# One product in four moved to TensorE in the middle layers of a four-layer state-space network

## The chip, the cores and the metric

The kernel runs on one core of one Trainium2 chip. The time is device microseconds of one execution of the whole program; three runs of the kernel before took 18013.67 to 18025.56 us, median 18020.86. The engines are named as in the profile: PE is TensorE (PEld its weight loads), DVE is VectorE, ACT is ScalarE, POOL is GpSimd, SP is SyncE, whose queue issues the DMAs.

## The reference

Four image layers on a batch of 4 images of 48 x 48 pixels and 192 channels, all in float32. Each holds selective scans. For a sequence of tokens t, channels d and N = 16 states n,

```
delta = softplus(dt @ dtW.T + dtB)
h[d,n] = exp(delta[d] * A[d,n]) * h[d,n] + (delta[d] * u[d]) * B[n]
y[d]   = sum over n of h[d,n] * C[n]      (+ D[d] * u[d])
```

Here u is the layer's input after a convolution, and dt, B and C are projections of it. Layers 0 and 3 are Mamba blocks with 384 channels, run forward and backward (layer 3 over every row and every column on its own, so that a scan starts anew every 48 tokens). Layers 1 and 2, the middle layers, run the scan over the whole image of 2304 tokens with 192 channels in four directions (rows, columns, and both reversed), add the four results, and normalize them.

## The kernel before

**Tiling.** A sequence is cut into chunks of CH = 384 tokens. One chunk of one direction of one image is a *job*; the middle layers have 2 x 4 x 4 x 6 = 192 jobs, of class DirJob (L536), all in one call of `run_jobs` (L1029). With 192 channels in blocks of 64, two halves of the states share the 128 partitions: partitions 0 to 63 hold 64 channels with states 0 to 7, partitions 64 to 127 the same channels with states 8 to 15 (`parts` = 2, `wide` = 64). So a job has 3 channel blocks i, and for each 2 *groups* g of NG = 4 states: 6 steps (i, g) a job, 1152 steps in the stage. Layers 0 and 3 use MambaJob (L588) with `parts` = 1: 12 steps a job.

**One step in the middle layers**, spread over engines and over neighbouring turns of the loop:

- *projection*: PE makes `bcd` (dt, B and C rows) from `xs`, ACT copies it, `spread` (L412) writes the 32 rows of B and C to DRAM (`bc`);
- *delta*: three PE products, each with a Softplus on ACT (`softplus`, L417);
- *fetch* (L422): SP loads the group's 4 B rows and 4 C rows back, each spread over 64 partitions, one DMA for each half: tile `bcb`, of which the pool holds 4;
- *decay* (L437): four Exp on ACT write `a` = exp(delta x A), into one of three buffers, two steps ahead;
- *drive* (L465): POOL makes `dus` = delta x xs; *enter* (L470): ACT copies it to `du` in PSUM, when a new i begins. In the middle layers it stands between the third and the fourth Exp of that turn;
- *carry* (L455): POOL copies the last state of the chunk before into the first column of the B rows, ahead of the product; `du` holds a 1 there;
- *scan* (L475): DVE multiplies `du` with the four B rows into `inputs` (PSUM, 4 x 385 elements a partition), and then runs the recurrence h = a x h + inputs over them in one scan instruction;
- *weigh* (L501): POOL copies the last column to `state` and multiplies h by the C rows, in place;
- *reduce* (L516): PE adds the four h to `y` in PSUM with a matrix of two stacked identities' sum (`pools.sum`); for a new i, `skip` (L561) first adds what the other directions left and D x u;
- *take* (L568), *gate* (L572), *close* (L577): ACT copies `y` to `yc`, PE adds its two halves to `ys`, ACT copies that to `o`, and after the third i SP stores it.

**Layers 0 and 3** differ in one thing that matters here: of the four products du x B of a group, MADE = 2 are made by PE (`fill`, L710). For that `du` is turned on PE (`turn`, L685, to `duT`), and the B row is brought in as a diagonal: `spread` (L641) writes the tokens of that row with 4-byte elements onto the diagonal of a zeroed DRAM block (`dg`), and `fetch` (L662) loads it to `bcb`. PE then multiplies `duT` by the diagonal blocks into PSUM tile `made`. DVE multiplies and scans only the other two states, and scans each made product with an instruction of its own, which takes its start from `state`.

**Order of the work.** DVE, POOL and PE execute in the order in which the program is written (`InOrder`), ACT through explicit dependencies (`in_order`). `run_jobs` writes that order: for each turn t it emits the scan of step t, decays of t+2, weigh of t, the next jobs' projections by slot (`stream`), the image ends' normalization by slot (`Side`: PE in slots 0, 4 and 5, POOL products in 0, 2, 4 and 5), gate, drive (of t+3 in the middle layers, t+4 in the others) and reduce. The number of a turn within its job is its slot, 0 to 5. In the middle layers reduce of t-1 is the last thing of a turn (`behind` = 1). `h` has 4 buffers, PSUM's eight banks hold `inputs` (4), `du`, `y` and two `ps` tiles for everything else.

Of the kernel before, what the change touches and what calls it, by code (L numbers as in the profile page):

```python
# [13 lines left out]
AF = mybir.ActivationFunctionType  # L14
# [7 lines left out]
Q = 96  # L22
CH = 384
# [5 lines left out]
MADE = 2  # L29
LINE = 3 * MADE * 128  # L30

# [30 lines left out]
class K:  # L62
# [100 lines left out]
    def mean_weights(self, n):  # L163
        w = self.tile(self.const, [Q, Q], f"mean{n}")
        self.nc.vector.memset(w, 1.0 / n)
        return w
# [82 lines left out]
class ScanPools:  # L249
# [6 lines left out]
    def __init__(self, k, ctx, parts, rows):  # L256
# [6 lines left out]
        self.made = parts == 1  # L263
# [9 lines left out]
        self.given = NG - MADE if self.made else NG  # L273
# [7 lines left out]
        if self.made:  # L281
            self.made_inputs = k.tile(self.vec, [128, 1024], "made")[:, 512 - CH : 512 + CH]
            self.n_jobs = 0
            self.diags = []
            zeros = self.decays[2].rearrange("p j l -> p (j l)")[:, : LINE + 1]
            k.g.memset(zeros, 0.0)
            for n in range(2 * self.groups):
                d = k.dram([128 * (LINE + 1)], "dg")
                k.nc.sync.dma_start(d.rearrange("(t x) -> t x", x=LINE + 1), zeros)
                self.diags.append(d)  # L290
# [41 lines left out]
class ScanJob:  # L332
# [16 lines left out]
    def turn(self, i):  # L349
        pass  # L350

    def turn_back(self, i):
        pass

    def fill(self, i, g):
        pass
# [55 lines left out]
    def spread(self):  # L412

        self.bc = self.k.dram([2 * N, self.pools.W], "bc")
        self.k.nc.sync.dma_start(self.bc, self.bcd[: 2 * N, :])

    def softplus(self, i, pd):  # L417
        if i == 0:
            self.delta = self.k.tile(self.pools.two, [128, 3, CH], "delta")
        self.k.act(self.delta[:, i, :], pd, AF.Softplus, bias=self.w.dtb[:, i, :])  # L420

    def fetch(self, g):  # L422

        k, pools = self.k, self.pools
        wide = pools.wide
        both = k.tile(pools.bcs, [128, 2, NG, pools.W], "bcb")
        self.bcb[g] = both[:, 0, :, :], both[:, 1, :, self.tokens]
        self.fetched[g] = []
        for m in range(pools.parts):
            at = (m * pools.groups + g) * 2 * NG  # L430
            ins = k.nc.sync.dma_start(
                both[m * wide : (m + 1) * wide].rearrange("p s j l -> p (s j l)"),
                self.bc[at : at + 2 * NG, :].rearrange("r l -> (r l)").partition_broadcast(wide),
            )
            self.fetched[g].append(ins)

    def decay(self, i, g, between=None):  # L437

        k, w, pools = self.k, self.w, self.pools
        if i == 0:  # L440
            self.fetch(g)
# [1714 lines left out]
```

## Time and profile before

| what | value |
|---|---|
| median of 3 runs | 18020.86 us |
| profiled execution | 18024.41 us, span 18022.6 us |
| busy share of the span | PE 90%, DVE 91%, ACT 76%, POOL 79% |
| granted TensorE clock, mean | 0.921 |
| middle layers, 6150 to 12135 us (5985 us) | PE 4672.44, DVE 5843.86, ACT 4359.13, POOL 4979.05 us busy; clock 0.80; DMA share 0.65 |
| ACT_TABLE_LOAD, 7000 to 11500 us | 2 x 143 of 1283 ns |
| delta on ACT, 7000 to 11500 us | 429 of 580 ns |

The shares of the whole span are a mean over stages with different limits: up to about 5.7 ms runs layer 0, then the input part of layer 1, from about 6.1 to 12.1 ms the scans of the middle layers, from 12.3 ms layer 3, and from about 17.3 ms the closing perceptron. The change is read from the middle stage.

A line of instruction groups holds the line of kernel.py, the engine, the operation, the tiles it writes and reads, shapes and count; behind the bar the busy time in us, the mean of one in ns, the idle time of the engine just before these instructions, and what ended most of that idle time. L59 is the helper that keeps program order, so groups are told apart by tiles. A line in order of time holds the start, the length, engine, line, operation and tiles, and in brackets idle time before it.

### The profile page before, as it was taken

What the parts mean: (1) busy time and instruction counts of PE and PEld (TensorE: products, weight loads), DVE (VectorE), ACT (ScalarE), POOL (GpSimd) and SP (SyncE); (2) the same over time, 40 slices, a digit from 0 to 9 for tenths busy, and PEclk for the clock granted to TensorE, in tenths of its full rate; (3) what the DMA queues carried; (4) which work ended last, traced back from release to release, by engine and by line L of the source; (5) the groups of instructions that cost most, each with busy time, mean ns of one, the idle gap of its engine ahead of it and who ended that gap; (6) DMA issues with size and microseconds to landing.
All of it is one profiled execution on the core that took longest, in us unless ns stands there. A gap on an engine that the chain in (4) does not pass through costs nothing. (4 is left out here: it accounts for less than half of the span.)

```text
span 18022.6 us, 313028 instructions
## 1 busy us (share of the span) xinstructions
PE 16243.2 (90%) x118512; PEld 10759.8 (60%) x118512; DVE 16418.0 (91%) x10747; ACT 13776.3 (76%) x25601; POOL 14149.0 (79%) x10862
## 2 busy tenths in 40 slices
PE   9999999999999777787777877878999999999999
PEld 7787787888885322222222222226888888888874
DVE  8899899999996799999999999996999999999992
ACT  7888888888885567777777777777888888888874
POOL 7877878878874488888888888876888888888880
PEclk9999999999999878788888887789999999999999
DMA  4343343333333466666666666663343343433431
GB/s 137 122 128 124 125 134 122 128 126 128 128 126 93 105 137 146 151 148 153 152 148 149 144 150 140 147 145 112 122 127 125 120 124 123 132 123 122 125 118 50
DMA packets 1229187, 2324.58 MB, mean 129 GB/s; under 512 B 704376, under 2 KB 962016, under 8 KB 1075232
## 3 DMA queue, kind: packets, MB, share of 16 engines
q1 hardware_dynamic: 1227680, 2304.55, 46.8%
q8 instruction: 938, 15.37, 0.4%
q14 instruction: 569, 4.66, 0.1%
HBM read 2105.57 MB, written 200.98 MB: 128 GB/s over the span
## 5 line engine op out<-in xcount | busy, mean ns | idle before, releaser
L59 POOL TENSOR_TENSOR h<-h,bcb 128x1536 f32<-128x1536 f32 x3456 | 11312.2, 3273 | 798.6 <-DVE h L59 499.1
L104 ACT ACTIVATE a<-delta,A 128x384 f32<-128x384 f32 (+1 forms) x13824 | 7377.6, 603 | 911.7 <-DVE h L59 901.2
L59 DVE TENSOR_TENSOR_SCAN h<-a,inputs 128x770 f32<-128x770 f32 (+2 forms) x3456 | 7915.9, 2290 | 146.5 <-DVE inputs L59 1.8
L59 DVE TENSOR_TENSOR inputs<-du,bcb 128x770 f32<-128x770 f32 (+2 forms) x3456 | 4256.4, 1232 | 287.2 <-POOL bcb L59 100.9
L59 PE MATMUL made<-bcb,duT 128*128 128x128 f32 x27648 | 3559.6, 279 | 172.1 <-DVE h L59 139.6
L59 PEld LDWEIGHTS y<-ident,h 128*128 128x128 f32 x27648 | 3119.8, 142 | 845.0 <-issue 485.7
L59 PE MATMUL y<-ident,h 128*128 128x128 f32 x27648 | 3508.5, 277 | 59.8 <-ACT yt L104 49.2
L59 PEld LDWEIGHTS made<-bcb,duT 128*128 128x128 f32 x27648 | 3341.4, 195 | 273.9 <-DVE h L59 178.7
L59 PE MATMUL y<-h,sum 128*64 128x384 f32 x9216 | 2661.7, 643 | 750.2 <-POOL h L59 547.4
L59 DVE TENSOR_TENSOR_SCAN h<-a,made 128x768 f32<-128x768 f32 (+1 forms) x1536 | 2343.2, 1536 | 263.2 <-PE made L59 256.4
L59 PEld LDWEIGHTS y<-h,sum 128*64 128x64 f32 x9216 | 848.7, 167 | 2175.9 <-issue 982.2
L59 DVE TENSOR_TENSOR_SCAN h<-a,state,made 128x384 f32<-128x384 f32 x1920 | 1827.8, 993 | 221.1 <-PE made L59 219.4
L59 POOL COPY state<-h 128x4 f32<-128x4 f32 x2304 | 434.4, 189 | 1908.5 <-DVE h L59 1879.5
L59 PE MATMUL ps<-bcd,dtT 12*128 12x384 f32 (+1 forms) x2304 | 1076.9, 580 | 245.1 <-ACT delta L104 240.2
L59 PE MATMUL ps<-u,inT 96*128 96x384 f32 x3456 | 1251.7, 489 | 38.8 <-DMA u<-xn_wh 27.1
L104 ACT ACTIVATE delta<-ps,vec 128x384 f32<-128x384 f32 x1152 | 636.4, 577 | 344.3 <-PE ps L59 338.2
L59 PEld LDWEIGHTS ps<-bcd,dtT 12*128 12x128 f32 (+1 forms) x2304 | 415.1, 206 | 808.8 <-ACT delta L104 487.3
L59 PE MATMUL ps<-yt,outT 128*96 128x384 f32 x2304 | 808.7, 488 | 0.4 <-POOL yt L59 0.4
L59 PE MATMUL ps<-xh,diag 32*32 32x192 f32 x32256 | 796.8, 324 | 4.0 <-ACT xc L104 2.3
L59 PEld LDWEIGHTS ps<-u,inT 96*128 96x128 f32 x3456 | 600.5, 191 | 304.0 <-issue 36.4
L104 ACT ACT_TABLE_LOAD x603 | 773.6, 1283 | 10.6
L101 ACT ACT_TABLE_LOAD x600 | 769.8, 1283 | 9.8 <-PEq L2146 0.7
(147 smaller groups left out, 15082.7 us busy)
## 6 DMA issues: line engine op xcount, KB each, us to landing
bcb<-bc SPq DMA_DIRECT2D x768, 770.0 KB
bcb<-bc SPq DMA_DIRECT2D x384, 1155.0 KB
bcb<-bc SPq DMA_DIRECT2D x384, 1152.0 KB
bcb<-dg SPq DMA_DIRECT2D x768, 384.0 KB
y<-o SPq DMA_DIRECT2D x192, 288.0 KB
xs<-xi_wh SPq DMA_DIRECT2D x96, 288.0 KB
xs<-xi_hw SPq DMA_DIRECT2D x96, 288.0 KB
added<-y SPq DMA_DIRECT2D x96, 288.0 KB
```

The source lines that it names most:

```text
L59: return lambda *a, **kw: self.tc.keep_in_program_order(op(*a, **kw))
L101: self.in_order(self.nc.scalar.preload_act_table_set(LOG_EXP))
L104: return self.in_order(self.nc.scalar.activation(out, in_, func, **kw))
```

## The change

In the middle layers PE makes one of the four products of each group (`MADE = {1: 2, 2: 1}`). The machinery of MambaJob (`spread`, `fetch`, `turn`, `fill`, `scan`) moves into ScanJob and is written for both values of `parts`. For a middle step this means:

- DVE multiplies and scans 3 x 385 elements instead of 4 x 385, and scans 384 made elements in a third instruction;
- PE turns the first 64 rows of `dus` (3 matmuls for each i) and makes the product with 6 matmuls of 128 columns (3 token blocks x 2 halves); reduce of t-1 is now followed by turn and then by fill of t+1; `inputs` takes three PSUM banks and `made` one;
- the fetch of a job's two groups is emitted two turns earlier (four steps ahead instead of two) and has a third DMA, the diagonal; `spread` writes one more row block and four diagonals;
- close, take and enter stand in front of the decays on ACT;
- the three deltas are copied with their bias and then go through one Softplus of 1152 elements, as in MambaJob;
- drive is emitted for t+4 instead of t+3; the result is copied into `added` (now three buffers) in place of `o`; `mean96` lives only in the input part of layer 1.

```diff
-MADE = 2
-LINE = 3 * MADE * 128
+MADE = {1: 2, 2: 1}
...
-        self.made = parts == 1
+        self.made = MADE[parts]
+        self.turned = parts == 1
+        self.line = 3 * self.made * parts * 128
...
-        self.given = NG - MADE if self.made else NG
+        self.given = NG - self.made
...
+        made = k.tile(self.vec, [128, 512 * self.made], "made")
+        at = 512 - CH if self.made == 2 else 0
+        self.made_inputs = made[:, at : at + self.made * CH]
...
     def spread(self):
-        self.bc = self.k.dram([2 * N, self.pools.W], "bc")
-        self.k.nc.sync.dma_start(self.bc, self.bcd[: 2 * N, :])
+        k, pools = self.k, self.pools
+        sync, parts, made = k.nc.sync, pools.parts, pools.made
+        n = parts * pools.groups * (pools.given + NG)
+        self.bc = k.dram([n, pools.W], "bc")
+        sync.dma_start(self.bc, self.bcd[:n, :])
+        be = k.dram([parts, pools.groups, made, CH], "be")
+        sync.dma_start(be.rearrange("m g e l -> (m g e) l"), self.bcd[n : 2 * N, self.tokens])
+        at = pools.n_jobs % 2 * pools.groups
+        pools.n_jobs += 1
+        self.lines = pools.diags[at : at + pools.groups]
+        for g in range(pools.groups):
+            line = self.lines[g].rearrange("(t x) -> t x", x=pools.line + 1)[:, : pools.line]
+            line = line.rearrange("t (b e m c) -> t b e m c", b=3, m=parts, c=128)
+            for e in range(made):
+                for m in range(parts):
+                    with k.nc.allow_non_contiguous_dma(reason="diagonal"):
+                        sync.dma_start(
+                            line[:, :, e, m, 0:1],
+                            be[m, g, e].rearrange("(b t v) -> t b v", t=128, v=1),
+                        )
 
     def softplus(self, i, pd):
...
-        self.k.act(self.delta[:, i, :], pd, AF.Softplus, bias=self.w.dtb[:, i, :])
+        k.act(self.delta[:, i, :], pd, AF.Identity, bias=self.w.dtb[:, i, :])
+        if i == 2:
+            k.act(self.delta, self.delta, AF.Softplus)
 
     def fetch(self, g):
...
+        k.nc.sync.dma_start(
+            t[:, n:], self.lines[g][: 128 * pools.line].rearrange("(t x) -> t x", t=128)
+        )
...
+    def turn(self, i):
...
+        for b in range(3):
+            k.t.matmul(
+                ps[:, b * wide : (b + 1) * wide],
+                self.du[i][:wide, b * 128 : (b + 1) * 128],
+                k.ident[:wide, :wide],
+                start=True,
+                stop=True,
+                is_transpose=True,
+                skip_group_check=True,
+            )
+        self.duT[i] = k.tile(pools.two, [128, 3, wide], "duT")
+        k.copy(self.duT[i].rearrange("p b d -> p (b d)"), ps)
+
+    def fill(self, i, g):
...
+        for b in range(3):
+            for e in range(pools.made):
+                at = e * CH + b * 128
+                for m in range(pools.parts):
+                    k.t.matmul(
+                        pools.made_inputs[m * wide : (m + 1) * wide, at : at + 128],
+                        self.duT[i][:, b, :],
+                        self.bcb[g][2][:, b, e, m, :],
+                        start=True,
+                        stop=True,
+                        skip_group_check=True,
+                    )
...
     def scan(self, i, g):
...
+        n = pools.given
+        du = pools.du.unsqueeze(1).to_broadcast([128, n, pools.W])
+        k.v.tensor_tensor(pools.b, du, self.bcb[g][0], ALU.mult)
...
+        scan(slice(0, n), slice(0, pools.W), pools.b.rearrange("p j l -> p (j l)"))
...
+        for e in range(pools.made):
+            at = g * NG + n + e
+            first = 0.0 if self.prev is None else self.prev.state[:, i, at : at + 1]
+            scan(
+                slice(n + e, n + e + 1),
+                self.tokens,
+                pools.made_inputs[:, e * CH : (e + 1) * CH],
+                first,
+            )
...
     def close(self, i):
-        if i == 0:
-            self.o = self.k.tile(self.pools.two, [64, 3, CH], "o")
-        self.k.copy(self.o[:, i, :], self.ys)
+        self.k.copy(self.added[:, i, :], self.ys)
...
-    behind = 2 if jobs[0].pools.made else 1
-    ahead, taken, gated, driven = 2, behind + 1, behind + 2, 2 + behind
+    behind = 2 if jobs[0].pools.turned else 1
+    ahead, taken, gated, driven = 2, behind + 1, behind + 2, 4
+    fetched = 2 * ahead if behind == 1 else ahead
...
-        coming = at_group(t + 1, 0)
-        if behind == 2:
-            if done := at_group(t - taken, last_group):
-                done[0].take(done[1])
-            if coming:
-                coming[0].enter(coming[1])
-                coming = None
+        if t + fetched < len(groups) and groups[t + fetched][1] == 0:
+            job, i, g = groups[t + fetched]
+            job.fetch(g)
+        if done := at_group(t - gated - 1, last_group):
+            done[0].close(done[1])
+        if done := at_group(t - taken, last_group):
+            done[0].take(done[1])
+        if coming := at_group(t + 1, 0):
+            coming[0].enter(coming[1])
         if t + ahead < len(groups):
             job, i, g = groups[t + ahead]
-            job.decay(i, g, (lambda: coming[0].enter(coming[1])) if coming else None)
-        if done := at_group(t - gated - 1, last_group):
-            done[0].close(done[1])
-        if behind == 1 and (done := at_group(t - taken, last_group)):
-            done[0].take(done[1])
+            job.decay(i, g)
...
-        if soon := at_group(t + 2, 0):
+        if behind == 2 and (soon := at_group(t + 2, 0)):
             soon[0].turn(soon[1])
...
         if 0 <= t - behind < len(groups) and behind == 1:
             job, i, g = groups[t - behind]
             job.reduce(i, g)
+        if behind == 1 and (soon := at_group(t + 2, 0)):
+            soon[0].turn(soon[1])
         if t + 1 < len(groups):
             job, i, g = groups[t + 1]
             job.fill(i, g)
```

## The prediction

> **What bounds the kernel now.** First the stretches of the span: busy time by engine (us and instructions, in the order PE, PEld, DVE, ACT, POOL), granted clock, DMA share, GB/s.
>
> ```profile
> 3000.00:4000.00 1000.00, 992.75 (x9001) 810.54 (x8999) 950.22 (x850) 837.24 (x1560) 797.13 (x760) 0.98 0.39 126
> 8000.00:9000.00 1000.00, 784.65 (x2484) 268.13 (x2484) 979.82 (x383) 732.64 (x1367) 841.95 (x721) 0.81 0.66 151
> 13000.00:14000.00 1000.00, 968.48 (x9845) 805.48 (x9843) 943.14 (x655) 816.37 (x1521) 864.51 (x436) 0.99 0.39 122
> ```
>
> Layers 0 and 3 (first and third row) are held by TensorE; they already make products there. The middle layers are held by VectorE, 98% busy. Next the groups of instructions by form, middle layers (7000 to 11500 us), then layer 0 (1000 to 5000 us).
>
> ```profile
> L59 POOL TENSOR_TENSOR h<-h,bcb 128x1536 f32<-128x1536 f32 x856 | 2948.4, 3444 | 69.5 <-POOL state L59 1.2
> L59 DVE TENSOR_TENSOR_SCAN h<-a,inputs 128x1540 f32<-128x1540 f32 x855 | 2873.6, 3361 | 32.9 <-DVE inputs L59 0.5
> L59 PE MATMUL y<-h,sum 128*64 128x384 f32 x6832 | 1971.0, 640 | 527.2 <-POOL h L59 374.0 <-POOL state L59 61.7 <-issue 42.9
> L59 DVE TENSOR_TENSOR inputs<-du,bcb 128x1540 f32<-128x1540 f32 x856 | 1515.2, 1770 | 78.8 <-POOL bcb L59 23.3 <-ACT du L104 13.7 <-PE y L59 12.2
> ```
>
> ```profile
> L59 POOL TENSOR_TENSOR h<-h,bcb 128x1536 f32<-128x1536 f32 x828 | 2410.8, 2912 | 66.8 <-POOL state L59 0.6
> L59 DVE TENSOR_TENSOR_SCAN h<-a,inputs 128x770 f32<-128x770 f32 x827 | 1453.0, 1757 | 30.1
> L59 DVE TENSOR_TENSOR_SCAN h<-a,state,made 128x384 f32<-128x384 f32 x1367 | 1301.4, 993 | 158.3 <-PE made L59 157.0
> L59 PE MATMUL made<-bcb,duT 128*128 128x128 f32 x9926 | 1290.9, 281 | 14.3 <-DVE h L59 11.2 <-DMA bcb<-dg 2.0
> L59 DVE TENSOR_TENSOR inputs<-du,bcb 128x770 f32<-128x770 f32 x828 | 797.1, 963 | 53.0 <-POOL bcb L59 52.3 <-DMA bcb<-bc 0.4
> ```
>
> The layer 0 rows are the price list of the new shape. Third, the order of time on VectorE, which shows what a mean hides: the distance from start to start. Middle layers, then layer 0:
>
> ```profile
> 8041.75 1.77 DVE L59 TENSOR_TENSOR inputs<-du,bcb 128x1540 f32<-128x1540 f32 x1
> 8043.55 3.36 DVE L59 TENSOR_TENSOR_SCAN h<-a,inputs 128x1540 f32<-128x1540 f32 x1
> 8046.95 1.77 DVE L59 TENSOR_TENSOR inputs<-du,bcb 128x1540 f32<-128x1540 f32 x1
> ```
>
> ```profile
> 3001.52 0.96 DVE L59 TENSOR_TENSOR inputs<-du,bcb 128x770 f32<-128x770 f32 x1
> 3002.51 1.76 DVE L59 TENSOR_TENSOR_SCAN h<-a,inputs 128x770 f32<-128x770 f32 x1
> 3004.19 1.89 DVE L59 TENSOR_TENSOR_SCAN h<-a,state,made 128x384 f32<-128x384 f32 x2
> 3006.01 0.96 DVE L59 TENSOR_TENSOR inputs<-du,bcb 128x770 f32<-128x770 f32 x1
> ```
>
> A quiet middle step is 8046.95-8041.75 = 5.20 us. The scan is followed 0.04 us after its end by the product that overwrites what it reads; in layer 0 the next instruction starts 0.08 before a scan's end (1.68 against 1.76). The stage has 1152 steps; from the first product at 6085.16 to the last at 12135.01 they took 6049.85/1151 = 5.256 each.
>
> Fourth, POOL in order of time, around its longest step:
>
> ```profile
> 8004.75 0.19 POOL L59 COPY state<-h 128x4 f32<-128x4 f32 x1 [0.41 <-PE y L59]
> 8005.02 3.45 POOL L59 TENSOR_TENSOR h<-h,bcb 128x1536 f32<-128x1536 f32 x1
> 8008.43 0.99 POOL L59 TENSOR_TENSOR nx<-nx,nsq 96x384 f32<-96x384 f32 x1
> 8009.38 0.99 POOL L59 TENSOR_TENSOR dus<-delta,xs 128x384 f32<-128x384 f32 x1
> 8010.32 0.18 POOL L59 COPY bcb<-state 128x4 f32<-128x4 f32 x1
> ```
>
> VectorE's products start at 8004.72 and 8010.55 here: the carry into bcb stands behind a norm's product and a drive, and the step grows to 5.83.
>
> **VectorE's own time.** Product: (1770-963)/770 = 1.048 ns an element, so 1155 elements take 963+385x1.048 = 1367 ns, plus the 0.03 gap: 1.40. Scan: (3361-1757)/770 = 2.083, so 2559 ns, less 0.08: 2.48. The scan of the made product: (3006.01-3004.19)/2 = 0.91. Sum 4.79, against 5.20: -0.41 a quiet step, -472 us over 1152. Measured from the mean of 5.256, which holds 0.06 of waits, a stage without any wait would save 537. That is the floor; the rest is what grows around it. (The chunk that opens a pass has no state, 935 ns in its row; left out, 0.01 a step.)
>
> **TensorE.** Added a step: 12 matmul instructions of 128 columns, and 3 turns every second step. PE is now busy 4672.44 us in 1138 steps (6150 to 12135), 4.11 each, at clock 0.80: 3.29 at full clock. Price of the 12: if the two 64-column halves overlap as in y<-h,sum, 1971.0/6832/3 = 0.096 each, 1.15 (0.93 at full clock); if they don't, layer 0's 1290.9/9926 = 0.130, 1.56. Turns: ps<-ident,dus took 101.6/621 = 0.164, so 0.25 a step. At full clock 4.47 to 5.06; at 0.81, 5.56 or more, over 5.20. So it hangs on the clock. It falls now because PE stands 374 us of the 4500 waiting for POOL's h; the fill sits in that hole, and a PE that falls behind is busy without a break, which in layers 0 and 3 goes with 0.98 and 0.99. I take about 0.9. The clock falls after short holes too: PE worked 0.22 us in 8018 to 8020, and the clock was 0.50 from 8020. The Trainium skill ("TensorE: Matmul & The Clock Gate", HAM oscillation in real kernels) says that the clock halves once PE idles for more than some 3.4 us. By that rule alone, gaps under 3.4 us would leave the clock full, the 0.08 below for half-clock steps would be 0, and the sum 4.96; since the trace halves it sooner, the sum goes by the rows.
>
> **The made wait.** made has one buffer: the fill may start when the scan of the made product ends, and must be done 1.40+2.48 = 3.88 later. It stands on PE behind reduce(t-1), which waits for POOL's weigh: from one scan's end, 0.28+3.44, then reduce 1.44 (8068.77 to 8070.21), turns 0.3, fill about 1: 6.5, where 4.79+3.88 = 8.67 is allowed; at half clock 9.1. That reduce can begin when weigh ends is the work of the moved take: PE's y<-added waits 274.9 us for ScalarE's yc today, because yc is copied behind the decays. Queued behind the waiting fill on PE are the next step's projections, gate and norm products, and behind those ScalarE's copies of them, which have until the next step. Bounds: 0, and layer 0's (158.3+48.0)/828 = 0.25, with only 0.99+1.68 of cover. Taken: 0.08, for half-clock steps.
>
> **POOL.** The drive moves from t+3 to t+4, so from odd to even steps, where slots 0, 2 and 4 also offer the norms' products; today they meet only in slot 5. The stage has 84+48+36 = 168 such products and 40 waits on bcb (27.7 us), the slot-5 ones. The other 128 or so, in even slots, now meet a drive, with the carry, and so VectorE's next product, queued behind both: each step 5.83 instead of 4.79, 128x1.04 = 133 us or 0.116 a step. The lower end: weigh at layer 0's 2912 ns (the C rows start at another offset in bcb there, and will here) makes it 5.30 and 0.057. Taken 0.10. The average load, 4.38 a step, fits.
>
> **SP and DMA.** Per job: one row write and four diagonal writes more, at 6.02/8 = 0.75 us of issue, 3 us ahead of the fetches, and two line loads. Behind the diagonals, which wait for the row write, stand the fetches, the next xs loads and the y store. Today the job whose bc leaves at 8050.74 issues its first fetch at 8052.40; the packets of its second end near 8069.6, and VectorE uses them at 8072.95: 3.3 us of room. The floor takes 5x0.41 = 2.1 of it, the diagonals about 2 (3.4 after bc instead of 1.66): some 1 us late a job at the floor, 0.2 a step; but waits of 0.2 a step elsewhere give it back. Bytes a group grow from 8x385 to 7x385+768 a partition, 12% on a share of 0.66. Bounds 0 and 0.20; taken 0.04. The fetches' earlier place in the program, past the y store and the side loads, gains nothing I can see: SP is held by bcd. Filling the zero lines costs some 10 us once, on the 20.83 before the first product.
>
> **ScalarE.** Three Identity for three Softplus of 0.58: nothing. The one Softplus is 1.16, duT 3x0.45: 2.5 a job on 3.83 a step, so 4.25 of 5. The du copy, now in front of the four decays, waits for VectorE's product (1.40) with those decays queued behind it; they are made two steps ahead, which covers it. The heavy pair of steps (slots 2 and 3: 8 Exp of 0.604, 3 deltas of 0.58, two table loads of 1.283, 1.16, 0.45, three copies of 0.48) is 12.2 us of work in 9.6, with du 1 us ahead of its use; if that cover goes, each job pays up to 1. Bounds 0 and 0.10; taken 0.03, today's (13.7+12.2)/855. Result copy into added, mean96's place: nothing, off every chain.
>
> **Sum.** 4.79+0.08+0.10+0.04+0.03 = 5.04; (5.256-5.04)x1152 = 249, less 10: -239. The profiled execution took 18024.41 (span 18022.6), 3.6 above the median: 17785. All upper ends make 5.46, +240 with the start: 18265. All lower ends make 4.85, -458: 17566.
>
> **Rivals.**
> 1. Nearly the floor: weigh at 2.91 and the fill hidden, 4.87 a step, 17590. For: 3.88 of cover. Against: the waits of layer 0 and 3. Chance 0.17.
> 2. The fetch chain or POOL paces the step at 5.25, so nothing is gained: 18027. For: 1 us of headroom lost, bursts at DMA share 1. Against: only 10 us of DMA waits today. 0.11.
> 3. Slower: PE becomes the bound because its clock stays at 0.81: 5.56 a step, +0.304x1152+10 = +360, 18385. It decides below a clock of 4.47/5.256 = 0.85. For: 0.80 now with PE 78% busy. Against: layers 0 and 3. 0.12.
>
> The forecast has 0.60, with its own range 17650 to 17920. Leaving out rival 3 and the tails gives 17590 to 18110. About 0.2% (36 us) is what can be told from no change: faster 0.60+0.17, same 0.07, slower 0.16.
>
> **What will show it.** VectorE: product near 1367, scan near 2559, 993 for the made one, quiet step 4.79. Wait on made under 0.1 a step. Waits of inputs on bcb near 115 us for POOL. Clock 0.9. Wrong if the quiet step is not 4.79, if the made wait is above 0.25, or if the clock stays at 0.81.

## The result and the profile after

The changed kernel takes 18085.82 us (median of five runs, 18051.15 to 18115.33) where the kernel before takes 18020.86 us. The ratio is 1.0036, 95% interval 1.0025 to 1.0047: 65 us slower, where 239 us faster was forecast. The profiled execution took 18088.52 us, span 18086.7 us. Layers 0 and 3 are as they were. In the middle stage the first product starts at 6083 us (before 6085) and the last at 12209 (before 12135): the mean step grew from 5.256 to 5.322 us.

First the stretch of the middle stage that answers to the second row of the first fence of the prediction (busy time of PE, PEld, DVE, ACT, POOL, granted clock, DMA share, GB/s), changed kernel:

```profile
8000.00:9000.00 1000.00, 860.40 (x4906) 397.86 (x4904) 883.21 (x554) 755.06 (x1442) 811.76 (x693) 0.91 0.70 159
```

VectorE fell from 98% to 88% busy, and the clock rose from 0.81 to 0.91. No engine is busy all the time any more: the stage is held by waits. The groups of instructions by form, 7000 to 11500 us, changed kernel:

```profile
L58 POOL TENSOR_TENSOR h<-h,bcb 128x1536 f32<-128x1536 f32 x842 | 2907.4, 3453 | 68.5 <-POOL state L58 0.8 <-PE ps L58 0.2
L58 DVE TENSOR_TENSOR_SCAN h<-a,inputs 128x1155 f32<-128x1155 f32 x842 | 2154.6, 2559 | 31.9
L58 PE MATMUL y<-h,sum 128*64 128x384 f32 x6728 | 1589.1, 557 | 426.8 <-POOL h L58 406.1 <-issue 8.8 <-POOL a L58 5.8
L58 DVE TENSOR_TENSOR inputs<-du,bcb 128x1155 f32<-128x1155 f32 x841 | 1148.4, 1365 | 225.8 <-POOL bcb L58 172.0 <-DMA bcb<-bc 20.9 <-POOL state L58 5.2
L58 PE MATMUL made<-bcb,duT 128*64 128x128 f32 x10092 | 794.8, 296 | 86.8 <-DMA bcb<-dg 82.7 <-DVE inputs L58 3.8
L58 DVE TENSOR_TENSOR_SCAN h<-a,state,made 128x384 f32<-128x384 f32 x697 | 691.5, 992 | 166.3 <-PE made L58 166.2
```

The durations on VectorE are the forecast ones (2559, 1365 and 992 ns). What is new stands behind the last bar: the product waits 172.0 us for POOL's carry, the scan of the made product waits 166.2 us for PE (called the *made wait* from here on), and PE's fill waits 82.7 us for the diagonal's load. A step without these waits is the forecast one too; VectorE in order of time:

```profile
8051.77 1.37 DVE L58 TENSOR_TENSOR inputs<-du,bcb 128x1155 f32<-128x1155 f32 x1
8053.17 2.56 DVE L58 TENSOR_TENSOR_SCAN h<-a,inputs 128x1155 f32<-128x1155 f32 x1
8055.64 0.99 DVE L58 TENSOR_TENSOR_SCAN h<-a,state,made 128x384 f32<-128x384 f32 x1
8056.56 1.37 DVE L58 TENSOR_TENSOR inputs<-du,bcb 128x1155 f32<-128x1155 f32 x1
```

From start to start 8056.56-8051.77 = 4.79 us.

For all profiles the idle stretches of 0.1 us and more ahead of VectorE's products and scans in the middle stage were added up by what ended them. Where a product waits for POOL's carry and the carry had itself waited for a DMA, the stretch counts as a fetch wait; "collision" is a carry that stood behind a norm's product and a drive, "carry" one that stood behind other work of POOL's. "Half" and "full" give the made wait by the clock in the 6 us ahead of it (mean under or over 0.75).

| us in the whole stage | before | after |
|---|---|---|
| made wait, half clock / full | 0 | 256 / 33 |
| fetch | 8 | 117 |
| POOL, collision / carry | 23 / 0 | 114 / 32 |
| ScalarE | 17 | 8 |
| PE's y | 13 | 0 |
| all | 69 | 574 |
| mean step; clock in the stage | 5.256; 0.803 | 5.322; 0.903 |

Without these waits the mean step fell from 5.256-69/1152 = 5.196 to 5.322-574/1152 = 4.824, which gave 429 us; the waits took 505 us more than before. Within a job, whose steps are counted 0 to 5, the made waits lie in steps 2 and 3, with 134 and 141 us. (The expectations up to e12 count the steps of the made waits one lower: their slots 1 and 2 are these. Their figures for one step in e7 and e10 are up to 6 us higher than the ones below, which hold the middle stage alone.) What is ahead of them shows in one job. First PE in order of time, changed kernel:

```profile
8019.22 1.51 PE L58 MATMUL y<-h,sum 128*64 128x384 f32 x8 [1.56 <-POOL h L58]
8020.67 0.40 PE L58 MATMUL ps<-ident,dus 64*128 64x64 f32 x3
8023.29 1.55 PE L58 MATMUL made<-bcb,duT 128*64 128x128 f32 x12 [2.22 <-DMA bcb<-dg]
8024.77 4.05 PE L58 MATMUL ps<-xs,xpT 64*38 64x384 f32 x6
8028.62 1.48 PE L58 MATMUL y<-added,ident 64*64 64x384 f32 x2
8030.03 2.83 PE L58 MATMUL y<-h,sum 128*64 128x384 f32 x8
8032.64 1.10 PE L58 MATMUL made<-bcb,duT 128*64 128x128 f32 x12
8033.67 2.49 PE L58 MATMUL ps<-bcd,dtT 6*128 6x384 f32 x6
...
8036.47 3.24 PE L58 MATMUL y<-h,sum 128*64 128x384 f32 x7
8039.64 0.54 PE L58 MATMUL ps<-ident,dus 64*128 64x64 f32 x3
8040.11 0.88 PE L58 MATMUL made<-bcb,duT 128*64 128x128 f32 x12
```

and VectorE in the same stretch:

```profile
8022.40 1.36 DVE L58 TENSOR_TENSOR inputs<-du,bcb 128x1155 f32<-128x1155 f32 x1 [1.97 <-POOL bcb L58]
...
8033.79 1.02 DVE L58 TENSOR_TENSOR_SCAN h<-a,state,made 128x384 f32<-128x384 f32 x1 [1.75 <-PE made L58]
...
8041.04 1.01 DVE L58 TENSOR_TENSOR_SCAN h<-a,state,made 128x384 f32<-128x384 f32 x1 [2.35 <-PE made L58]
```

PE stands 2.22 us for the late diagonal; then its clock is halved, and the projection takes 4.05 us (2.12 at full clock), the reduction 2.83 (1.51). The next fill is late, and VectorE waits 1.75 us at 8033.79. Then, although PE has been busy without a break since 8023.29, the reduction behind the delta products takes 3.24 us again, and VectorE waits 2.35 us at 8041.04. This second half clock had no idle time ahead of it; experiment e13 looks for its cause.

The clock falls in spells of 3.41 us, some of them several times as long, 228 in the changed kernel from 6150 to 12135 us. In the 3.42 us ahead of 148 of them PE was idle for more than 1.3 us. In 76 it was idle for under 0.3 us, and in every one of these 76 windows lies a delta product (ps<-bcd,dtT), which uses 6 or 12 of the 128 rows.

### The profile page after: what moved, and what is told of

Read it like the earlier page. It is cut to its first block, busy times and chain, and to the rows that moved or that the text cites. A ratio compares the mean times of both kernels' runs of the same rounds, so it can differ in the third digit from the quotient of the medians.

```text
span 18086.7 us, 346872 instructions
## 1 busy us (share of the span) xinstructions
PE 16804.4 (93%) x134064; PEld 11603.4 (64%) x134064; DVE 16026.6 (89%) x11899; ACT 14067.4 (78%) x26369; POOL 14142.9 (78%) x10863
## 5 line engine op out<-in xcount | busy, mean ns | idle before, releaser
L58 DVE TENSOR_TENSOR_SCAN h<-a,inputs 128x770 f32<-128x770 f32 (+2 forms) x3456 | 6992.1, 2023 | 146.0 <-DVE inputs L58 1.4
L58 PE MATMUL made<-bcb,duT 128*128 128x128 f32 (+1 forms) x41472 | 4647.0, 285 | 289.1 <-DVE h L58 141.2
L58 PEld LDWEIGHTS made<-bcb,duT 128*128 128x128 f32 (+1 forms) x41472 | 4221.4, 180 | 692.9 <-issue 299.1
L58 DVE TENSOR_TENSOR inputs<-du,bcb 128x770 f32<-128x770 f32 (+2 forms) x3456 | 3790.5, 1097 | 467.3 <-POOL bcb L58 282.0
L58 DVE TENSOR_TENSOR_SCAN h<-a,state,made 128x384 f32<-128x384 f32 x2880 | 2781.0, 993 | 451.1 <-PE made L58 449.6
L58 DVE TENSOR_TENSOR_SCAN h<-a,made 128x768 f32<-128x768 f32 (+1 forms) x1728 | 2522.3, 1469 | 314.7 <-PE made L58 307.5
L58 PE MATMUL y<-h,sum 128*64 128x384 f32 x9216 | 2184.3, 558 | 611.1 <-POOL h L58 582.7
L58 PEld LDWEIGHTS y<-h,sum 128*64 128x64 f32 x9216 | 707.5, 147 | 1722.4 <-POOL h L58 892.7
L103 ACT ACTIVATE duT<-ps 128x384 f32<-128x384 f32 (+1 forms) x1152 | 468.6, 407 | 1065.6 <-PE ps L58 1062.8
L58 PE MATMUL ps<-bcd,dtT 12*128 12x384 f32 (+1 forms) x2304 | 961.3, 524 | 50.1 <-ACT delta L103 41.9
L100 ACT ACT_TABLE_LOAD x600 | 769.8, 1283 | 10.2 <-PEq L2109 0.7
```

Of the source, the lines that this page charges most:

```text
L58: return lambda *a, **kw: self.tc.keep_in_program_order(op(*a, **kw))
L100: self.in_order(self.nc.scalar.preload_act_table_set(LOG_EXP))
L103: return self.in_order(self.nc.scalar.activation(out, in_, func, **kw))
```

## The experiments

All times are medians; ratios are to the kernel before, run on the same chip beside them. The last columns are us in the middle stage, counted as above.

| run | what | us | ratio, 95% interval | made | fetch | POOL | clock |
|---|---|---|---|---|---|---|---|
| after | the change | 18086 | 1.0036 [1.0025, 1.0047] | 289 | 117 | 146 | 0.903 |
| e1 | entry column by ScalarE | 17956 | 0.9962 [0.9947, 0.9977] | 201 | 62 | 146 | 0.917 |
| e2 | drive at t+3 | 18442 | 1.0234 [1.0218, 1.0249] | 497 | 335 | 49 | 0.871 |
| e3 | e1 and e2 | 18404 | 1.0213 [1.0196, 1.0230] | 411 | 344 | 53 | 0.878 |
| e4 | unread matmuls in four slots | 18370 | 1.0197 [1.0181, 1.0212] | 665 | 53 | 46 | 0.972 |
| e5 | xs load behind the fetches | 18011 | 1.0002 [0.9992, 1.0012] | 313 | 38 | 145 | 0.907 |
| e6 | e5 and drive at t+3 | 18021 | 1.0008 [0.9997, 1.0018] | 404 | 40 | 89 | 0.894 |
| e7 | e1, e5, diagonals behind the first rows | 17858 | 0.9911 [0.9896, 0.9925] | 176 | 1 | 157 | 0.925 |
| e8 | no made product | 18079 | 1.0033 [1.0020, 1.0046] | 0 | 9 | 70 | 0.798 |
| e9 | e7 and unread matmuls in slot 0 | 17850 | 0.9908 [0.9893, 0.9922] | 164 | 2 | 159 | 0.949 |
| e10 | e7 and drive at t+3 | 17790 | 0.9874 [0.9859, 0.9889] | 133 | 3 | 95 | 0.932 |
| e11 | e10, third delta a slot later | 17870 | 0.9914 [0.9898, 0.9931] | 215 | 3 | 111 | 0.923 |
| e12 | after without fill | 18100 | 1.0047 [1.0032, 1.0062] | 0 | 155 | 140 | 0.801 |
| e13 | e10, delta over all rows | 17724 | 0.9836 [0.9819, 0.9852] | 101 | 1 | 88 | 0.951 |
| e14 | e13 and unread matmuls in slot 0 | 17718 | 0.9836 [0.9821, 0.9851] | 89 | 2 | 84 | 0.976 |
| e15 | e7 without fill | 18123 | 1.0060 [1.0045, 1.0075] | 1 | 114 | 146 | 0.805 |

In e12 and e15 a further 204 and 182 us are waits for which the profile names no releaser; 51 of these 55 waits in e12 and 43 of 45 in e15 end just behind ScalarE's copy into du.

### e1 to e4: one suspected wait each

e1 lets ScalarE write the zero of bcd's entry column, which POOL wrote behind its longest step:

```diff
-                k.g.memset(self.bcd[:, self.entry : self.entry + 1], 0.0)
+                first = self.bcd[:, self.entry : self.entry + 1]
+                if pools.parts == 2:
+                    k.act(first, px[:, :1], AF.Copy, scale=0.0)
+                else:
+                    k.g.memset(first, 0.0)
```

> The changed kernel with one edit: in the middle layers the zero in the entry column of bcd is written by ScalarE next to its own copy, not by POOL behind weigh, so that the row write, the diagonals and the fetches start some 4 us earlier (the trace of the changed kernel has a median of 3.97 us between ScalarE's copy and the row write). In that trace VectorE waits about 571 us in the stage: 288 for the made product (275 of it in slots 1 and 2, 256 with the clock at half), 146 for the carry behind POOL's own work, 114 for late fetches. Theory A (three separate costs): the fetch waits of 114 us go to under 15, the made wait falls by no more than 30; time -0.5% to -0.8%, some 17960 us. Rival B (late fetches empty PE, its clock falls, and the made waits follow from that): 107 us of the made waits lie within 18 us after a fetch wait and go too; time -1.0% to -1.3%, some 17870 us. Rival C (fetches are limited by DMA rate, not by their start): nothing changes, within 0.2%.

It took 17956 us, 0.9962 of before, and so beat both kernels. In the changed kernel the write of bc left a median 3.5 us after the end of ScalarE's copy into bcd, because it also waits for POOL's memset, and that stands behind weigh; in e1 it left after 0.1 us. Fetch waits fell from 117 to 62 us and made waits from 289 to 201. So the time is theory A's by luck: it had the fetch waits under 15 us and at most 30 us off the made waits. That a late fetch costs part of the made waits behind it, as rival B says, fits this run; e5 below shows that it is no rule.

e2 puts the drive back to t+3 (`driven = 2 + behind`), e3 does both.

> The changed kernel with the drive of the middle layers put back to t+3, so into odd steps. Theory A: the 114 us of carries that stand behind a norm's product and a drive, and the 32 us of carries behind a drive alone, fall to about 30 and 30; time -0.3% to -0.5%, some 18010 us. Rival (POOL's lag is only moved: the odd steps' carry waits instead, or the made wait takes its place): within 0.2% of the changed kernel, 18050 to 18110 us.

> Both edits together. Theory A: the gains add, -0.9% to -1.2% against the changed kernel, some 17880 us, so faster than the kernel before by 0.6% to 0.9%. If they share a cause, the sum is less than the two alone.

The collisions went (114 to 10 us, e2), as the count of steps said, but the time rose by 356 us: fetch waits 335 us, made waits 497 us. e3 shows the same (18404 us, fetch waits 344, made waits 411): the gains did not add. The reason is on SP. Its queue is in one order, laid down with the program, and there the load of xs for the job after next stood between the write of be and the diagonals in 133 of 188 jobs (43 in the changed kernel). That load waits for the drive that last reads the old xs, which now came a step later; the diagonals and fetches stood behind it. SP in order of time, e2:

```profile
8095.43 0.53 SPq L414 DMA_DIRECT2D bc<-bcd  x1
8096.01 0.29 SPq L416 DMA_DIRECT2D be<-bcd  x1
8096.35 0.58 SPq L624 DMA_DIRECT2D xs<-xi_wh  x1
8098.77 2.58 SPq L426 DMA_DIRECT2D dg<-be  x4
8101.51 1.14 SPq L454 DMA_DIRECT2D bcb<-bc  x2
```

The first fetch leaves 6.08 us after bc. In the other order, which 128 of the 188 jobs of the changed kernel have, it leaves 1.61 us after bc (median), but its second half stands behind the four diagonals, at 4.8 us.

e4 gives PE five matmuls of 128 columns, whose results nothing reads, in unused columns of the bank of made, ahead of reduce, in slots 0, 3, 4 and 5.

> The changed kernel with idle work on TensorE: five matmuls of 128 columns into unused columns of made's bank ahead of reduce in slots 0, 3, 4 and 5 of the middle layers, about 1.1 us a step at full clock, put where PE waits for weigh. It computes nothing that is used. Theory A (the made waits are PE's half clock in slots 1 and 2): granted clock in the middle layers from 0.90 to 0.96 or more, made waits from 288 us to under 120, time -0.6% to -1.0%, some 17950 us, although PE has about 770 us more to do. Rival (PE has too much to do in slots 1 and 2 at any clock): made waits as before or larger, time 0 to +1%.

The clock rose to 0.972, but the time to 18370 us. As a test of the clock it failed by its own making: the bank is that which VectorE scans, and PE waited for that scan. The group in e4, 7000 to 11500 us:

```profile
L58 PE MATMUL made<-ident 128*128 128x128 f32 x5370 | 744.5, 286 | 334.3 <-DVE h L58 334.3
```

### e5 to e8: the order on SP, and the change without its product

e5 orders the load of xs behind the last fetch of the job before; e6 is e5 with the drive at t+3.

```diff
-            k.nc.sync.dma_start(self.xs[m * 64 : (m + 1) * 64], self.part(self.src))
+            ins = k.nc.sync.dma_start(self.xs[m * 64 : (m + 1) * 64], self.part(self.src))
+            k.behind(ins, self.pools.fetched)
```

> The changed kernel with one thing more: the load of a job's xs is ordered behind the job before's last fetch on SP's queue. In the changed kernel 43 of 188 jobs have an xs load between the write of be and the diagonals, and there the first fetch leaves 4.45 us after bc instead of 1.61 us, and VectorE's product waits 2.08 us a job instead of 0.84 us. Theory Q (the order on SP's queue makes the fetches late): no job is left in which the xs load stands there, and 43 x 1.24 = 53 us of product waits go, with some made waits behind them: 18000 to 18040 us. Theory C (the made wait comes from TensorE's clock and work alone, and the fetches follow other things): 18070 to 18100 us, as before this edit.

> The same order of the xs load, with the drive back at t+3, as in the run that came out at 18442 us. There 133 of 188 jobs had the xs load between be and the diagonals, and it waited for POOL's drive, so that the first fetch left 6.1 us after bc. Theory Q: that is all that was wrong with the drive at t+3; the fetch waits fall from about 321 to below 110 us, POOL's collisions stay gone, and the time is 17900 to 18000 us. Theory D (a drive one step later is itself too late, for turn or for du): the time stays above 18300 us although the queue's order is that of the run beside it.

In both no job is left with an xs load ahead of its diagonals. e5 stands at 1.0002 of before where the changed kernel stands at 1.0036, some 65 us, as theory Q had it; its fetch waits fell from 117 to 38. The made waits did not fall with them (313 us for 289), although the fill's wait for the diagonals did (20.4 us for 82.7, 7000 to 11500 us). PE's waits for the load of xs, which now stands behind the fetches, rose from 14 to 57 us in the stage; whether that holds the made waits up was not tried. e6 came down from 18442 to 18021 us: the order on the queue explains most of the loss of e2. But the made wait of e6 is 404 us against 313 in e5, and so the 56 us taken from POOL's waits came back as more, and theory Q's 17900 to 18000 was missed. That PE's lag had been hidden behind POOL's collisions would explain it, but is not shown; e10 goes the other way.

e7 joins e5 and e1 and issues the diagonals only behind both halves of the first group's rows:

```diff
             self.fetched[g].append(ins)
+        if pools.parts == 2 and g == 0:
+            self.diagonals()
```

> The xs order, the zero of the entry column written by ScalarE, and the diagonals put behind both halves of the first group's B and C rows on SP's queue (in the changed kernel the second half stands behind the four diagonals and leaves 4.8 us after bc). Theory Q: the second half leaves 2.3 us after bc, product waits for DMA fall from 59 us (entry column alone) to 30 us or less, made waits fall with them from 201 us to about 150 us: 17850 to 17910 us. Rival: the line's load, now 1 us later, makes the fill late instead; waits of the fill on DMA grow above 100 us and the time stays at 17950 us or more.

17858 us, as theory Q had it. SP in order of time, e7:

```profile
8059.00 0.34 SPq L431 DMA_DIRECT2D bc<-bcd  x1
8059.39 0.30 SPq L433 DMA_DIRECT2D be<-bcd  x1
8060.58 1.11 SPq L480 DMA_DIRECT2D bcb<-bc  x2
8061.74 2.70 SPq L450 DMA_DIRECT2D dg<-be  x4
8064.55 0.56 SPq L480 DMA_DIRECT2D bcb<-bc  x1
```

From the end of ScalarE's copy into bcd to the second half of the first fetch it takes a median 2.2 us now (8.5 in the changed kernel, 7.5 in e1, 7.8 in e5). Fetch waits are 1 us, and PE's fill waits 1.1 us for the diagonals (82.7 in the changed kernel, 7000 to 11500 us), so that their later place costs nothing. The made wait is 176 us.

e8 is the changed kernel with `MADE = {1: 2, 2: 0}`.

> The changed kernel without the made product in the middle layers (VectorE multiplies and scans all four states again; no diagonals, turn or fill there); the early fetch, the new order on ScalarE, the one softplus and the drive at t+4 stay. Theory P (these parts give back what they save): VectorE's waits of 67 us in the kernel before lose the 30 us behind y and du, and the drives at even steps add 128 collisions of about 0.6 us with the norms' products, 80 us: 18040 to 18100 us. Rival (ScalarE's new order is worth something by itself): 17960 to 18000 us.

18079 us, as theory P had it: everything but the product makes the kernel slower than before, by 64 us. VectorE's product in e8, 7000 to 11500 us:

```profile
L58 DVE TENSOR_TENSOR inputs<-du,bcb 128x1540 f32<-128x1540 f32 x845 | 1495.4, 1770 | 133.6 <-POOL bcb L58 67.8 <-ACT du L103 30.0 <-ACT a L103 5.2
```

The wait for POOL's carry is 67.8 us (23.3 before): the drive at even steps. The waits for PE's y went (13 to 2 us in the stage), but those for ScalarE rose from 17 to 52 us. So on top of the other parts the product with its fill, diagonals and turn neither wins nor loses measurably (1.0033 without it, 1.0036 with it).

### e9 to e12: what makes the made wait

e9 is e7 with 12 unread matmuls in slot 0, this time into y's bank, ahead of a reduce that adds to an open y, so that they wait for PE alone.

> The kernel of the run with the diagonals behind the first group's rows (17857 us), and in slot 0, where no norm product is given to TensorE, 12 matmuls of 128 columns into unused columns of y's bank ahead of reduce; nothing reads them and nothing but TensorE touches that bank then. In the changed kernel 113 of the 248 stretches of 1.5 us and more in which TensorE stands idle lie in slot 0, ahead of the projections of slots 1 and 2. Theory C (the half clock that follows these holes makes the made wait): cold made waits of 151 us fall to 80 us or less, mean clock of the stage from 0.92 to 0.94 or more, time 17770 to 17810 us. Theory W (the amount of work ahead of the fill makes it, at any clock): clock up, but made waits stay at 190 us or grow, 17850 to 17950 us.

The clock rose to 0.949 and the made wait of step 2 fell from 64 to 13 us; that of step 3 rose from 103 to 130 us, and the time stayed (17850 us). So theory C holds for step 2, but step 3 has another cause: of this run's 164 spells 111 begin with under 0.3 us of PE idle ahead of them, all with a delta product there.

> The kernel of 17857 us with the drive back at t+3. Theory S (a wait taken from POOL's collisions comes back as made wait, because TensorE has then less time): the carry's waits behind a norm's product and a drive fall from 118 us to about 40 us, made waits rise from 191 us to 240 us or more, time 17820 to 17870 us. Rival (the two add): made waits stay at 191 us, 17770 to 17800 us.

With the fetches on time the drive at t+3 does gain, 68 us: collisions fell from 118 to 38 us, and made waits fell too (176 to 133) where theory S had them rise. Why e6 and e10 differ in this was not tried.

> The kernel with the drive at t+3 of the run beside it, and the third delta product with the one softplus moved from slot 2 to slot 3. Theory W: the made wait in slot 2 (109 us in the kernel of 17857 us) comes from the projections there; one of three moved away halves it, slot 3 gets 20 us at most, and the time is 40 to 70 us under the run beside it. Rival: the softplus a step later makes POOL's drive or the Exp late; POOL's waits for delta (24 us in 4500 us) rise above 60 us and the time is equal or higher than that of the run beside it.

Slower by 80 us than e10. The made wait of step 3 went from 79 us to nothing, but step 0 got 115 us and step 5 36 us. PE's waits for ScalarE's copies for the norms rose (7000 to 11500 us: for nsq from 7.0 us in e10 to 106.3, for turned from 6.2 to 38.5); that ScalarE makes these copies late because the softplus comes a step later is likely, but not shown. The rival's place was wrong (POOL's wait for delta is 28 us), its sign right.

> The changed kernel without the fills of the middle layers but the first: the made input keeps old data, so that the product of one state in four is not the right one; diagonals, lines and turn stay. Theory T (TensorE's fill is what costs the gain, by itself and by what it pushes): the made waits of 288 us go, the waits for DMA (114 us) and for POOL (146 us) stay or grow a little: 17780 to 17850 us, near the time that was forecast. Rival F (the late fetches start it all and the made waits only show them): the fetch waits grow by what the made waits lose, and the time stays above 17950 us.

18100 us. The made wait was gone and nothing was gained; rival F's number holds, yet fetch waits rose only from 117 to 155 us. The run is no clean test of the fill: with it gone the order on SP's queue moved as well, and the xs load stands ahead of the diagonals in 32 jobs more than in the changed kernel.

### e13 to e15: rows, holes and the fill

e13 lets the delta products of e10 run over all 38 or 44 rows of bcd; the added rows of the weights are zero:

```diff
         self.dtT = k.tile(pool, [nr, 3, 128], f"dtT{tag}")
+        if parts == 2:
+            nc.vector.memset(self.dtT[: 2 * N], 0.0)
...
-                lambda ps: (ps, [(w.dtT[2 * N : nr, i, :], self.bcd[2 * N : nr, self.tokens])]),
+                lambda ps: (ps, [(w.dtT[low:nr, i, :], self.bcd[low:nr, self.tokens])]),
```

> The kernel of 17790 us (diagonals behind the first group's rows, drive at t+3), with the delta products over all 38 or 44 rows of bcd instead of its last 6 or 12; the added rows of the weights are zero, so the result and the number and width of the matmuls stay. In that kernel 76 half-clock spells begin with under 0.3 us of TensorE idle in the 3.42 us ahead of them, and all 76 have a delta product there. Theory R (a product of 6 or 12 rows does not hold the clock): such spells fall to 20 or fewer, the made wait of slot 3 from 84 us to 30 us or less, time 17710 to 17760 us. Rival (the rows do not matter, or zero weights count as nothing): about 76 spells again and 17770 to 17810 us.

17724 us, 66 us under e10. Half clock spells with under 0.3 us of idle ahead of them fell from 76 to 1 (6150 to 12135 us, as above; the one lies behind the middle stage). Delta products, reduction and fill of one job in order of time, in e10:

```profile
8006.46 2.49 PE L58 MATMUL ps<-bcd,dtT 6*128 6x384 f32 x6
...
8009.27 2.66 PE L58 MATMUL y<-h,sum 128*64 128x384 f32 x7
...
8012.37 1.36 PE L58 MATMUL made<-bcb,duT 128*64 128x128 f32 x12
```

and in e13:

```profile
8007.90 2.49 PE L58 MATMUL ps<-bcd,dtT 38*128 38x384 f32 x6
...
8010.80 1.67 PE L58 MATMUL y<-h,sum 128*64 128x384 f32 x8
...
8012.73 0.88 PE L58 MATMUL made<-bcb,duT 128*64 128x128 f32 x12
```

The products themselves take the same 2.49 us; what comes behind them no longer runs at half clock. The made wait of step 3 fell from 79 to 35 us. The spells that are left in e13 all have a hole: in each of the 119 in its middle stage PE was idle for more than 1.3 us of the 3.42 us ahead. e11 agrees from another side: there the six delta matmuls stand as four and two, and no spell begins with under 0.3 us of idle. The edit also moves the products from row 32 of the array to row 0, so that the number of rows and their place are not separated. All this is shown on e10; on the changed kernel itself the rows alone were not tried.

> The same and the 12 unread matmuls in slot 0. Theory R with C (both kinds of half clock make the made wait, the one of slot 2 from the hole in slot 0, the one of slot 3 from the few rows): made waits of slots 2 and 3 together fall from 130 us to 40 us or less, mean clock of the stage 0.96 or more, time 17670 to 17730 us. Rival (the added work pushes the made wait to slot 3, as in the run with the unread matmuls alone): slot 3 above 100 us, 17770 us or more.

The clock rose to 0.976, half clock made waits fell from 55 to 16 us, but those at full clock grew from 46 to 73 us, and the time is that of e13. The range was met, but not as theory R with C had it: steps 2 and 3 together went from 77 us in e13 to 47, and the time did not move. A higher clock bought with added work gains nothing there.

> The kernel of 17857 us without the fills of the middle layers but the first (one product in four is then not the right one). In the changed kernel leaving them out gained nothing, and the fetch waits grew instead. Theory K (two limits stand behind each other, the fetch chain and then TensorE's fill): with the chain mended, the fetch waits stay below 30 us, the made waits of 191 us go, and the time is 17640 to 17720 us. Rival (a third limit, ScalarE or POOL, takes the place of the made wait): waits for du, a or POOL grow by 100 us or more, 17780 us or more.

18123 us: the kernel of 17858 us became slower by leaving work out of PE. But the edit moved more than PE's work. In 23 jobs a load of rows for the norms (nr<-zs) now stands ahead of bc on SP's queue and waits for POOL's product for the norms, so that bc leaves a median 10.2 us after the end of ScalarE's copy into bcd; in e7 it leaves within 1 us in every job. One such job in order of time, e15:

```profile
7964.24 0.54 ACT L103 ACTIVATE bcd<-ps 38x1 f32<-38x1 f32 x2
...
7973.14 0.99 POOL L58 TENSOR_TENSOR nx<-nx,nr 96x384 f32<-96x384 f32 x1
...
7974.16 0.34 SPq L1528 DMA_DIRECT2D nr<-zs  x1
7974.60 0.39 SPq L431 DMA_DIRECT2D bc<-bcd  x1
...
7990.41 2.51 SPq L652 DMA_DIRECT2D xs<-xi_wh  x2
...
7994.98 0.19 POOL L58 COPY bcb<-state 128x3 f32<-128x3 f32 x1 [4.77 <-DMA bcb<-bc]
7995.21 1.37 DVE L58 TENSOR_TENSOR inputs<-du,bcb 128x1155 f32<-128x1155 f32 x1 [3.72 <-POOL bcb L58]
...
7998.65 4.03 PE L58 MATMUL ps<-xs,xpT 64*38 64x384 f32 x6 [6.30 <-DMA xs<-xi_wh]
```

VectorE waits 3.72 us for the late fetch, and PE 6.30 us for the late xs, with the next projection behind it. These jobs lie between 6957 and 9785 us. The steps 96 to 671 of the stage, which hold them but for the last, took 252 us more than the same steps in e7, all others together 2 us more. So the loss goes with the order on SP's queue, as in e2, and not with the clock, which is low in the whole stage (0.805, as in e12, e8 and the kernel before: without the fill PE has holes again). From 10000 to 11500 us, where no such job lies, VectorE waits 86 us in all at a clock of 0.84, and in e7 91 us at 0.94, 42 of them for made: without the fill these go and others come in their place. What leaving out the fill alone is worth stays open. The rival's number holds, and waits behind du did grow, but the queue that the runs show behind it was in neither theory.

## Why the prediction was wrong, point by point

**VectorE's own time: right.** 1365, 2559 and 992 ns against 1367, 2559 and 993; the quiet step is 4.79.

**TensorE: right.** Clock 0.903 for 0.9; the 12 matmuls took 794.8/10092 x 12 = 0.95 us for 0.93 to 1.15. The holes do halve the clock before 3.4 us are reached: of 137 stretches of 1.5 to 2.0 us without PE, 72 were followed by a half clock within 4 us, and only 4 of all were longer than 3.4. The prediction's own row for this (8018 to 8020 us) is not clean, since delta products of 6 rows stand ahead of that hole; e13 is, and there 79 of 118 stretches of 2.0 to 2.5 us were followed by a half clock. "TensorE: Matmul & The Clock Gate" of the Trainium skill (Part 1: The HAM clock gate) has the clock set by a free-running window of about 3.4 us. The spells of 3.41 us agree with the window; they do not agree with a gap of 3.4 us as the condition.

**The made wait: the step that failed.** Taken 0.08 a step, measured (256+33)/1152 = 0.25, the upper bound. Two things were wrong. "Queued behind the waiting fill on PE are the next step's projections", it said, and let them have until the next step: but they stand ahead of the next fill. The 6.5 us (9.1 at half clock) that were set against the 8.67 allowed hold the reduction, but neither the projection, 4.05 us at half clock, nor the skip, 1.48. And the half clock was charged to holes alone; the delta products of few rows bring it with PE busy. Of the 289 us of made wait 256 have half clock ahead of them: e9 took most of step 2's away by filling holes, e13 more than half of step 3's by the rows. How much late diagonals add, which the prediction gave to SP only, stays open: e1 and e5 both cut the fill's wait for them (82.7 us) to 29.6 and 20.4, and the made waits fell by 88 us in one and rose by 24 in the other.

**POOL: nearly right.** Taken 0.10, measured 114/1152 = 0.10 for 108 collisions of 1.05 us (128 of 1.04 forecast), and 0.03 for carries behind a drive alone. Weigh did not become faster: 3453 ns, so the lower end was no possibility.

**SP and DMA: undersized.** Taken 0.04, measured 117/1152 = 0.10. The forecast order (row write, diagonals, fetches) is not the one that the queue has. In 43 jobs an xs load stands there as well; in nearly all, bc waits for POOL's memset, a median 3.5 us behind ScalarE's copy. The statement that waits elsewhere give the lateness back did not hold: with 457 us of other waits in the stage the fetches still cost 117. In e1 55 us of fetch waits went together with 88 us of made waits, so that lateness can even be paid twice; in e5 it was not.

**ScalarE and the start: harmless.** ScalarE 8/1152 = 0.01 for 0.03. The first product came 2 us earlier, not 10 later. Without the made product the same parts cost more there (e8: 52 us of waits for ScalarE, 17 in the kernel before); the one softplus was not tried alone.

**Sum.** With the measured sizes 4.79+0.25+0.13+0.10+0.01 = 5.28; a further 14 us of waits and the gaps under 0.1 us make it 5.32. None of the rivals came true: the clock was not 0.81 (rival 3), and neither the fetch chain nor POOL alone held the step (rival 2). It was the forecast's own sum, with the made wait three times and the fetch wait two and a half times its size.

**What the mechanism was worth.** With the fetch chain mended (e7), the drive at t+3 (e10) and the delta over all rows (e13) the same made product gives 17724 us, 0.9836 of before; the step is 5.005, where 5.04 was forecast. These edits without the product can't be what gained this: the kernel before has 69 us of waits in all, and e13 is 290 us faster than the runs of it beside. VectorE's groups in e13, 7000 to 11500 us:

```profile
L58 DVE TENSOR_TENSOR inputs<-du,bcb 128x1155 f32<-128x1155 f32 x898 | 1226.2, 1366 | 86.6 <-POOL bcb L58 39.6 <-POOL state L58 7.4 <-ACT du L103 4.1
L58 DVE TENSOR_TENSOR_SCAN h<-a,state,made 128x384 f32<-128x384 f32 x750 | 743.5, 991 | 57.5 <-PE made L58 57.0
```

## What to carry to other kernels

When a change takes 8% off the engine that bounds a stage, list every chain that has less than that much room, and count the work that an in-order engine does for later steps as standing ahead of the next deadline, not behind this one: a price from one step's view is too low. A DMA chain is only as early as its slowest releaser and its place in its queue; look for a memset, a load of another job or a diagonal that stands in it, and read the queue's order from the trace, not from the program's text. That holds for experiments too: a run that only leaves work out can move the order on a queue, and then its time says little about that work (e12, e15).

## What the runs showed of the hardware that was not expected

- A busy TensorE can lose its clock. Some 2.5 us of matmuls that use 6 or 12 of 128 rows were followed by half clock within 3.4 us in 81 of 195 cases in the changed kernel and in 77 of 192 in e10; with 38 or 44 rows, the added weights all zero, in none of 192 (e13). The matmuls themselves take as long either way.
- Less work on TensorE lowered its clock: without the fill the clock in the stage fell from 0.925 to 0.805 (e7, e15). The time that e15 lost is not shown to come from that.
- Matmuls into unused columns of a PSUM bank waited for another engine's read of other columns of that tile: 334 us in 4500 (e4). The profile infers such a wait from a semaphore, so it is one that the program makes; what the chip does without it was not tried.
- POOL's weigh takes 3453 ns in the middle layers with the C rows at the new offset, as before (3444), and 2912 in layer 0. The cause is open.
